# The last norm, the value tiles and the residual of a two-layer graph transformer, emitted as chains of their own

## The chip, the cores and the metric

The kernel runs on one core of a Trainium2 chip. The core has five engines that each work through their own queue in the order in which the program was written: TensorE (PE; weight loads are shown apart as PEld), VectorE (DVE), ScalarE (ACT), GpSimd (POOL) and SyncE (SP), which here only issues DMAs. They wait for each other by semaphores. The metric is the device time of one launch in microseconds; all times below are in microseconds unless they say ns. Samples are processed one after the other on this core; nothing is shared with other cores.

## What is computed

The input has 16 samples of 1024 nodes with 256 features and a 1024 x 1024 adjacency of zeros and ones. Each sample goes through two layers. Cut to what matters:

```python
# layer 0: typed graph attention, 4 heads of 64
h = einsum('bnd,hde->bhne', x, W)
attention = softmax(where(adj == 0, -1e9, leaky_relu(e_src + e_dst)))
dst = einsum('bhij,bhje->bhie', attention, h) + bias
x = layernorm(x + head_norm(relu(dst) + h))
# layer 1: attention with q = k = v, 8 heads of 32, then an MLP
normed = layer_norm(x) * gamma1 + beta1
attn = softmax(where(adj > 0, normed @ normed.T / sqrt(32), -inf))
y = layer_norm(x + attn @ normed) * gamma2 + beta2
x1 = x + attn @ normed
x = layernorm(x1 + gelu(y @ W1 + b1) @ W2 + b2)     # the last norm
```

All of it is in fp32.

## The kernel before

**Two layers side by side.** The kernel is one long straight program that a planner in Python writes out while it runs. Two generators, `layer0` and `layer1`, each emit one sample after the other: layer 0 of sample b+1 is interleaved with layer 1 of sample b. Each `yield` in them says how much work was emitted and what the next piece needs. The main loop picks the stream that comes next: `wanted()` interpolates in `COURSE` (L1095) how far layer 0 should have come for the place that layer 1 has reached, and the loop takes layer 0 while it is behind that target. `WORK0` (L1088) is the sum of work of one sample's layer 0; `SLACK1` and `STAY` (L1093, L1094) say how far the loop may leave the target when the piece at hand would have to wait. A rough clock (`Pace`) estimates when each engine would be free and each tile written; the order is fixed when the program is built.

**A sample's layer 0.** `prepare` projects the nodes in eight blocks of 128. Each is two matmuls acc<-w0e,xT of 128 x 264, which this text calls projection halves; ScalarE then makes a mask out of the adjacency (mask<-ak) and takes four small pieces out of the bank (apart, v, dinv, hb), and VectorE makes z and v. `attention0` (32 steps of two blocks) lets VectorE make weights (p<-cb,dinv,mask) three steps ahead and TensorE multiply them with the values (acc<-v,p, sixteen records per block as an fp32 product is two passes). Its results are read by a chain (`residual0`: a reciprocal, relu, hb), then `after0` normalises.

**A sample's layer 1.** `attention1` has 32 steps. Each makes logits for four heads (ps<-nT, eight records, into the four banks of the pool `ps`), ScalarE takes exponentials out of them (p<-ps, four of 128 x 512), VectorE multiplies by the mask (p<-p,mask, two of 128 x 1024), and three steps later TensorE multiplies by the values v1 (po<-p,v, po<-p,unit, po<-v,p). When the 16 steps of one half of the queries are done, `half_done` starts `finish1` (o<-o,x, statistics, x<-x,o, then ScalarE's o and the transposes to yT). Then `mlp` works in pieces of two blocks: ps<-yT,w_sb, ScalarE's gelu (hid), po<-w_sb,hid; and `last_norm` per block: zz<-po,x on VectorE, after the second block of two the statistics, r on GpSimd (an addition and a power), t on VectorE, zz<-zz,t,r on ScalarE and a store.

**Chains.** Everything that follows a matmul and isn't itself a step is a chain: a generator that stops before each piece that needs something from another engine. `begin` puts it into a list; `advance` runs, between steps, every chain whose needs are met by the rough clock. `complete` runs a chain to its end at once, wherever it stands: its instructions then stand in the queues even if what they read is far from ready.

**What completes a chain early.** A chain is noted as a user of every tile that it takes (`born`) and that it was begun with. When a pool of n buffers hands out a tile for the (n+1)th time, `Ring.tile` (L73) calls `settle` (L450) for the tile whose place it takes, and that completes all chains that use it:

```python
        if len(taken) >= self.bufs:
            self.pace.settle(taken[-self.bufs])
```

So the chain of `last_norm` (L1014) is completed when the pool `po` (two banks) comes back to the bank that its addition read, and the chain of `after0` (L706), which took a bank of `acc` or `ps` for the transposes of normed (its tile is called sq, the transposed one nT), is completed when that bank is taken again. The tail of `after0` behind these transposes makes v1 (a memset and four products, v<-sq,g_r), ratio (two small products) and, 12 us later by the rough clock, the residual x1 (four, x<-sq,ratio,be_r). `half(n)` (L1062) gives `attention1` nT, v1 and x1 of a half of the nodes; if they aren't there it calls `finish_norms` (L1032), which completes all the half's norm chains.

Of the kernel before, what the change touches and what calls it, by code (L numbers as in the profile page):

```python
# [31 lines left out]
F32 = mybir.dt.float32  # L32
# [7 lines left out]
P = 128  # L40
# [150 lines left out]
def fast_path(  # L191
# [24 lines left out]
    nc = Pace(tc.nc)  # L216
    B, N, D = x.shape
    H0, _, HO = w0.shape
# [3 lines left out]
    HD = D // H1  # L222
    NB = N // P
# [4 lines left out]
    BPH = HALF // P  # L228
# [3 lines left out]
    PAIR = 2  # L232
    GB = 2
# [29 lines left out]
    unit = const.tile([P, Q], F32, name="unit")  # L263
# [26 lines left out]
    at = one.tile([P, 3, PAIR, HO, T], F32, name="v0")  # L290
# [38 lines left out]
    def at_time(t):  # L329
        return lambda: t  # L330
# [127 lines left out]
    def begin(chain, engine, *needs):  # L458
        for n in needs:
            if not callable(n):  # L460
                uses(chain, n.tensor.name)
        chains.append([chain, engine, needs])
# [22 lines left out]
    def complete(chain):  # L485

        for item in list(chains):
            if item[0] is chain:
                while item in chains:
                    run(item)  # L490
# [215 lines left out]
    def after0(b, n, hd, o):  # L706


        for first in range(hd + 1):
            complete(residuals[b, n, first])  # L710
        rowwise = [P, BPH, D]
        heads = slice((hd - PAIR + 1) * HO, (hd + 1) * HO)
        oh = o[:, :, heads].rearrange("p g (h e) -> p g h e", e=HO)
        per_head = [P, BPH, PAIR, HO]
        s = small.tile([P, BPH, PAIR], F32, name="s0")
        nc.vector.tensor_reduce(s, oh, axis=mybir.AxisListType.X, op=OP.add)
        nc.vector.scalar_tensor_tensor(
            oh, s[:, :, :, None].to_broadcast(per_head), -1.0 / HO, oh, op0=OP.mult, op1=OP.add
        )
        yield "scalar", o  # L720
        sq = two.tile([P, BPH, PAIR * HO], F32, name="oT1")
        nc.scalar.activation(sq, o[:, :, heads], AF.Square)
        if hd == H0 - 1:
            xl = one.tile(rowwise, F32, name="xl")
            load_x(xl, b, n * BPH, BPH)
        yield "vector", sq
        v = small.tile([P, BPH, PAIR], F32, name="v0s")
        nc.vector.tensor_reduce(
            v, sq.rearrange("p g (h e) -> p g h e", e=HO), axis=mybir.AxisListType.X, op=OP.add
        )  # L730
        r = rstd(v.rearrange("p g e -> p (g e)"), BPH * PAIR, EPS_HEAD * HO, "r0")
        r = r.rearrange("p (g e) -> p g e", e=PAIR)
        pair = o[:, :, heads]
        nc.vector.tensor_mul(pair, pair, lng0_r[:, None, heads].to_broadcast([P, BPH, PAIR * HO]))
        if hd == H0 - 1:
            nc.vector.tensor_add(xl, xl, lnb0_r[:, None, :].to_broadcast(rowwise))
        yield "vector", r
        nc.vector.tensor_mul(oh, oh, r[:, :, :, None].to_broadcast(per_head))
        if hd < H0 - 1:
            return  # L740
        complete(norms[b, n, PAIR - 1])
        nc.vector.tensor_add(o, o, xl)
        yield "vector", o
        mv = small.tile([P, BPH, 2], F32, name="mv0")
        statistics(o, mv, BPH)

        v2 = small.tile([P, 1, BPH], F32, name="v2")
        nc.vector.tensor_scalar(v2[:, 0, :], mv[:, :, 1], 1.0 + EPS, EPS * EPS, op0=OP.mult, op1=OP.add)  # L750
        r2 = power(v2[:, 0, :], BPH, "r2")
        r3 = rstd(mv[:, :, 1], BPH, EPS, "r3")
        yield "vector", r2
        t = minus_mean(mv[:, :, 0], r2, BPH)
        yield "scalar", t
        normed = one.tile(rowwise, F32, name="sq")
        scale_shift(normed, o, t, r2, BPH)
        yield "tensor", normed, side_ready
        nT = two.tile([P, DC, HALF], F32, name="nT")
        for g in range(0, BPH, GB):  # L760
            transpose_rows(nT[:, :, g * P : (g + GB) * P], normed[:, g : g + GB, :], g1_c, be1_c)
            yield "tensor", normed, side_ready
        yield "vector", normed
        v1 = two.tile([P, BPH, H1, HD + 1], F32, name="v1")
        nc.vector.memset(v1[:, :, :, HD], 1.0)
        for g in range(BPH):
            nc.vector.tensor_mul(
                v1[:, g, :, 0:HD],
                normed[:, g, :].rearrange("p (h e) -> p h e", e=HD),
                g1_r.rearrange("p (h e) -> p h e", e=HD),  # L770
            )
        handed[b, n] = [None, v1, nT]
        yield "vector", r3

        ratio = small.tile([P, BPH], F32, name="ratio")
        nc.vector.tensor_mul(ratio, v2[:, 0, :], r2)
        nc.vector.tensor_mul(ratio, ratio, r3)
        yield "vector", ratio, at_time(nc.now() + 12.0)

        x1 = three.tile(rowwise, F32, name="x1")  # L780
        for g in range(BPH):
            nc.vector.scalar_tensor_tensor(
                x1[:, g, :], normed[:, g, :], ratio[:, g : g + 1], be1_r, op0=OP.mult, op1=OP.add
            )
        handed[b, n][0] = x1


    def attention1(half, mask, rinv, half_done, rest):

# [34 lines left out]
                nc.vector.tensor_mul(p, p, mask[n][:, jb, None, :].to_broadcast([P, PAIR, HALF]))  # L826

        def products(quad, jb, ps, moved, held):
            values = half(jb // BPH)[1][:, jb % BPH, :, :]
            for e in range(PAIR):  # L830
                hd = quad * QUAD + e
                for at, v in ((e, values[:, hd, 0:HD]), (PAIR + e, unit)):
                    nc.tensor.matmul(
                        moved[at * Q : (at + 1) * Q, :], v, ps[0][:, e, :], start=jb == 0, stop=jb == NB - 1
                    )
            for e in range(PAIR):
                hd = quad * QUAD + PAIR + e
                for q in range(BPH):
                    for at in range(0, P, Q):
                        nc.tensor.matmul(  # L840
                            held[at : at + Q, q, e, :],
                            ps[1][:, e, q * P + at : q * P + at + Q],
                            values[:, hd, :],
                            start=jb == 0 and e == 0 and q == 0,
                            stop=jb == NB - 1 and e == PAIR - 1 and q == BPH - 1,
                        )
# [167 lines left out]
    def last_norm(b, k, g, po, x1, z, mv, first=None):  # L1014
        if first is not None:
            complete(first)
        nc.vector.tensor_add(z[:, g, :], po, x1)
        if g < GB - 1:
            return
        statistics(z, mv, GB)  # L1020
        r = rstd(mv[:, :, 1], GB, EPS, "r")
        yield "vector", r
        t = minus_mean(mv[:, :, 0], r, GB)
        yield "scalar", t
        scale_shift(z, z, t, r, GB)
        nc.sync.dma_start(out[b, k * P : (k + GB) * P, :].rearrange("(g p) d -> p g d", p=P), z)


    handed = {}
    norms, residuals = {}, {}  # L1030

    def finish_norms(b, n):  # L1032
        for chain in [c for at, c in norms.items() if at[:2] == (b, n)]:
            complete(chain)

    place = [[0, 0.0], [0, 0.0]]

# [18 lines left out]
    def layer1():  # L1056
        rest, ranges = iter(()), None
        for b in range(B):
            place[1][:] = b, 0.0 if b else REST1
            seen, rinv1, mask = handed.pop(b)  # L1060

            def half(n):  # L1062
                if (b, n) not in handed:
                    finish_norms(b, n)
                return handed[b, n]

            yT = [two.tile([P, DC, HALF], F32, name="yT") for _ in range(NH)]
            halves = {}

            def half_done(n, o, heads):  # L1070
                finish_norms(b, n)
                x1 = handed[b, n][0]
                chain = finish1(o, x1, yT[n], heads)
                bias = add_bias2(x1)
                halves[n] = x1, yT[n], chain, bias
                begin(chain, "vector", done(heads), o)
                begin(bias, "vector", at_time(nc.now() + 60.0), x1)

            yield from attention1(half, mask, rinv1, half_done, rest)
            complete(weights_of_later)  # L1080
            rest = yield from mlp(b, halves)
            in_range(seen)
        yield from rest
# [1 line left out]

    WORK0 = NB // GB * 2.25 + 2.0 + NB * H0 * 1.0  # L1088
    REST1 = 3.5 * GB
    ATTN1 = REST1 + 2.0 + 2.5 * (NH * NB * H1 // QUAD)  # L1090
    WORK1 = ATTN1 + NB // GB * (1.75 * FC / 2 + 3.5 * GB) - REST1
    SLACK = 0.083
    SLACK1 = 0.02  # L1093
    STAY = 0.017  # L1094
    COURSE = [(0.0, 1.0), (REST1 + 1.0, 1.0), (ATTN1, 1.31), (WORK1 - 12.0, 2.0), (WORK1, 2.0)]  # L1095

    def wanted():
        b, done = place[1]
# [478 lines left out]
```

## Time and profile before

| what | value |
|---|---|
| median of 3 runs | 3255.43 (3252.06 to 3255.72) |
| device time of the profiled execution | 3255.19 |
| its span from first to last instruction | 3253.4 |
| mean granted TensorE clock | 0.992 |
| mask products p<-p,mask on VectorE | 1024, mean 1220 ns |
| exponentials p<-ps on ScalarE | 2006 and 42 out of other banks, mean 612 ns |
| layer-0 weights p<-cb,dinv,mask on VectorE | 1024, mean 747 ns |
| x<-sq,ratio,be_r (x1) on VectorE | 128, mean 480 ns |
| v<-sq,g_r (v1) on VectorE | 128, mean 412 ns |
| zz<-zz,t,r on ScalarE | 128, mean 601 ns |
| activation table loads | 32, mean 1283 ns |

A row of the profile's groups names the engine, the operation, the tile written and the tiles read, and counts them. In the order of time a line has its start in us from the span's start, its length, and at the end, in brackets, how long the engine sat idle before it and what ended that. A line of several instructions runs from the first one's start to the last one's end. Buffer numbers are left out, so `acc` is either of two banks, `ps` one of four, `po` one of two. Nearly every operation carries the line of one helper (L61), so this text goes by tiles.

### The profile page before, as it was taken

How to read it: one execution, taken by the hardware profiler on the slowest of the kernel's cores; microseconds unless marked ns; L12 is line 12 of the kernel's file. 1: busy time of each engine (PE TensorE's matmuls, PEld its weight loads, DVE VectorE, ACT ScalarE, POOL GpSimd, SP SyncE). 2: the span in 40 equal slices, each digit the busy share in tenths (PEclk: the TensorE clock that was granted, in tenths of full speed). 3: DMA queues.
4: the chain of work that ended last, by engine and by line, in shares of the span. 5: the costliest groups of instructions: out<-in, count | busy, mean ns of one | idle time of the engine just before them, and what ended most of it. 6: DMA issues, size and time to landing. Idle time of an engine off the chain costs nothing.

```text
span 3253.4 us, 147229 instructions
## 1 busy us (share of the span) xinstructions
PE 3168.4 (97%) x67297; PEld 1979.3 (61%) x67297; DVE 2882.5 (89%) x4943; ACT 1961.9 (60%) x4256; POOL 511.3 (16%) x462
## 2 busy tenths in 40 slices
PE   5899999999999999999999999999999999999998
PEld 4557565575756657566575755757566575665745
DVE  5899898998989989898998989989898998989992
ACT  2473846748376583856738466483755838567483
POOL 1202112030110202112030120301102021120300
PEclk9799999999999999999999999999999999999999
DMA  7212202122031221303122031220312213011000
GB/s 169 58 38 59 63 26 67 39 63 52 26 85 21 70 46 32 87 20 73 36 66 56 26 74 33 63 52 25 87 26 68 41 42 80 20 44 21 30 7 16
DMA packets 209447, 163.18 MB, mean 50 GB/s; under 512 B 138480, under 2 KB 189680, under 8 KB 207856
## 3 DMA queue, kind: packets, MB, share of 16 engines
q1 hardware_dynamic: 204640, 119.07, 14.8%
q0 software_dynamic: 2592, 33.56, 5.3%
q8 instruction: 529, 8.67, 1.1%
q10 hardware_dynamic: 1584, 1.05, 0.1%
q14 instruction: 102, 0.84, 0.1%
HBM read 138.68 MB, written 48.50 MB: 58 GB/s over the span
## 4 chain that ended last, share of the span: by engine, by line
PE 75%; DVE 16%; ACT 4%; issue 3%; DMA 1%; POOL 0%; ACTq 0%; SPq 0%; POOLq 0%; DVEq 0%
PE po L61 28%; PE ps L61 28%; PE acc L61 19%; DVE p L61 14%; ACT p L61 2%; ACT o L61 0%; ACT nT L61 0%; DMA cb<-esr 0%; DVE o L61 0%; DVE st L61 0%; ACT zz L61 0%; DVE v L61 0%; DVE hb L61 0%; DVE z L61 0%; DVE relu L61 0%
## 5 line engine op out<-in xcount | busy, mean ns | idle before, releaser
L61 DVE TENSOR_TENSOR p<-p,mask 128x1024 f32<-128x1024 f32 x1024 | 1191.2, 1220 | 6.9 <-ACT p L61 6.9
L61 ACT ACTIVATE p<-ps 128x512 f32<-128x512 f32 x2006 | 1042.4, 612 | 235.9 <-PE ps L61 220.0
L61 DVE SCALAR_TENSOR_TENSOR p<-cb,dinv,mask 128x512 f32<-128x512 f32 x1024 | 709.3, 747 | 8.1 <-DMA cb<-esr 7.8
L61 PE MATMUL ps<-nT 32*128 32x512 f32 x4012 | 647.1, 641 | 2.2 <-ACT p L61 0.4
L61 ACT ACTIVATE hid<-ps,b_sb 128x256 f32<-128x256 f32 x512 | 242.0, 474 | 586.1 <-PE ps L61 586.1
L61 PE MATMUL acc<-v,p 128*64 128x65 f32 x16384 | 563.5, 225 | 31.0 <-DVE p L61 21.9
L61 PEld LDWEIGHTS po<-v,p 128*32 128x32 f32 x32768 | 397.3, 109 | 315.7 <-issue 264.6
L61 PEld LDWEIGHTS acc<-v,p 128*64 128x64 f32 x16384 | 536.7, 140 | 75.1 <-issue 14.4
L61 PE MATMUL po<-p,v 128*32 128x512 f32 x2048 | 543.4, 605 | 1.3 <-DVE p L61 1.3
L61 PE MATMUL po<-p,unit 128*32 128x512 f32 x2048 | 543.5, 605 | 0.0
L61 PE MATMUL po<-w_sb,hid 128*64 128x256 f32 x4096 | 476.2, 380 | 0.0
L61 PE MATMUL ps<-yT,w_sb 128*64 128x256 f32 x4096 | 475.7, 380 | 0.0
L61 POOL TENSOR_SCALAR r<-mv 128x4 f32<-128x4 f32 (+1 forms) x128 | 86.5, 676 | 2057.4 <-DVE mv L61 2019.5
L61 PE MATMUL po<-v,p 128*32 128x33 f32 x32768 | 393.1, 198 | 7.2 <-issue 6.7
L61 PEld LDWEIGHTS po<-w_sb,hid 128*64 128x64 f32 x4096 | 281.3, 137 | 146.3 <-issue 14.5
L61 PEld LDWEIGHTS ps<-yT,w_sb 128*64 128x64 f32 x4096 | 283.6, 137 | 135.4 <-issue 5.2
L61 POOL TENSOR_TENSOR r<-r,mhalf 128x8 f32<-128x8 f32 (+2 forms) x192 | 313.6, 1633 | 16.0
L61 PEld LDWEIGHTS ps<-nT 32*128 32x128 f32 x4012 | 201.9, 183 | 131.7 <-ACT p L61 84.5
L61 PEld LDWEIGHTS po<-p,v 128*32 128x32 f32 x2048 | 77.8, 108 | 321.7 <-issue 143.4
L61 DVE TENSOR_TENSOR z<-hb,bias_r 128x256 f32<-128x256 f32 x128 | 54.2, 423 | 163.8 <-ACT hb L61 163.8
L61 PE MATMUL acc<-w0e,xT 128*128 128x264 f32 x512 | 174.5, 435 | 10.5 <-issue 10.5
L61 ACT ACTIVATE mask<-ak,shift_c 128x1024 uint8<-128x1024 bf16 x120 | 142.1, 1184 | 0.0
(115 smaller groups left out, 2437.7 us busy)
## 6 DMA issues: line engine op xcount, KB each, us to landing
cb<-esr SPq DMA_DIRECT2D x64, 512.0 KB
adjb<-in_adj_dram POOLq DMA_DIRECT2D x30, 1024.0 KB, 11.5
xk<-in_x_dram SPq DMA_DIRECT2D x64, 256.0 KB
xl<-in_x_dram SPq DMA_DIRECT2D x32, 512.0 KB
out_dram<-zz SPq DMA_DIRECT2D x64, 256.0 KB
ak<-adjb SPq DMA_TRANSPOSE x240
ak<-in_adj_dram POOLq DMA_DIRECT2D x8, 256.0 KB, 6.8
w_sb<-in_L_gnn_W_dram SPq DMA_DIRECT2D x2, 1024.0 KB
```

Source lines behind the costliest of these rows:

```text
L61: return method(*args, **kwargs)
```

## The change

The tail of `after0` behind the last transposes of normed becomes two generators of their own, `values1` (v1) and `rows1` (ratio and x1), which `after0` begins when it ends; they took no bank, so no bank that comes back completes them. The hand-over `handed[b, n]` is filled with nT already there, v1 and x1 follow. `attention1` asks for v1 by a function of its own, `values(n)`, when the products need it, and `half(n)` completes only the chain that makes nT. `finish_norms` goes through its list twice, as completing `after0` puts new chains into it. In `last_norm` everything behind the second addition becomes the generator `norm_rows`, begun there with the tile z. The addition of b2 to x1 (`add_bias2`, x<-x,b_r) is due 70 instead of 60 us later by the rough clock, and five constants of the planner change.

```diff
@@ after0 @@
             yield "tensor", normed, side_ready
-        yield "vector", normed
+        handed[b, n] = [None, None, nT]
+        norms[b, n, "values"] = values1(b, n, normed)
+        begin(norms[b, n, "values"], "vector", normed)
+        norms[b, n, "rows"] = rows1(b, n, normed, v2, r2, r3)
+        begin(norms[b, n, "rows"], "vector", normed, r3)
+
+    def values1(b, n, normed):
         v1 = two.tile([P, BPH, H1, HD + 1], F32, name="v1")
...
-        handed[b, n] = [None, v1, nT]
-        yield "vector", r3
-
+        handed[b, n][1] = v1
+        yield from ()
+
+    def rows1(b, n, normed, v2, r2, r3):
         ratio = small.tile([P, BPH], F32, name="ratio")
         nc.vector.tensor_mul(ratio, v2[:, 0, :], r2)
         nc.vector.tensor_mul(ratio, ratio, r3)
         yield "vector", ratio, at_time(nc.now() + 12.0)
...
@@ attention1, products @@
-            values = half(jb // BPH)[1][:, jb % BPH, :, :]
+            v1 = values(jb // BPH)[:, jb % BPH, :, :]
...
@@ last_norm @@
         nc.vector.tensor_add(z[:, g, :], po, x1)
-        if g < GB - 1:
-            return
+        if g == GB - 1:
+            begin(norm_rows(b, k, z, mv), "vector", z)
+        yield from ()
+
+    def norm_rows(b, k, z, mv):
         statistics(z, mv, GB)
         r = rstd(mv[:, :, 1], GB, EPS, "r")
         yield "vector", r
...
@@ finish_norms @@
-        for chain in [c for at, c in norms.items() if at[:2] == (b, n)]:
-            complete(chain)
+        for _ in range(2):
+            for chain in [c for at, c in norms.items() if at[:2] == (b, n)]:
+                complete(chain)
...
@@ layer1 @@
                 if (b, n) not in handed:
-                    finish_norms(b, n)
+                    complete(norms[b, n, H0 - 1])
                 return handed[b, n]
+
+            def values(n):
+                if handed[b, n][1] is None:
+                    complete(norms[b, n, "values"])
+                return handed[b, n][1]
...
-                begin(bias, "vector", at_time(nc.now() + 60.0), x1)
+                begin(bias, "vector", at_time(nc.now() + 70.0), x1)
...
-    WORK0 = NB // GB * 2.25 + 2.0 + NB * H0 * 1.0
+    WORK0 = NB // GB * 2.0 + 2.0 + NB * H0 * 1.0
...
-    SLACK1 = 0.02
-    STAY = 0.017
-    COURSE = [(0.0, 1.0), (REST1 + 1.0, 1.0), (ATTN1, 1.31), (WORK1 - 12.0, 2.0), (WORK1, 2.0)]
+    SLACK1 = 0.01
+    STAY = 0.01
+    COURSE = [(0.0, 1.0), (REST1 + 0.0, 1.0), (ATTN1, 1.32), (WORK1 - 14.0, 2.0), (WORK1, 2.0)]
```

More of the change, by code (lines that the diff above doesn't have):

```diff
@@ L778, in after0 @@
         yield "vector", ratio, at_time(nc.now() + 12.0)
-        x1 = three.tile(rowwise, F32, name="x1")
+        x1 = three.tile([P, BPH, D], F32, name="x1")
         for g in range(BPH):
@@ L785, in after0, with attention1 @@
         handed[b, n][0] = x1
-    def attention1(half, mask, rinv, half_done, rest):
+    def attention1(half, values, mask, rinv, half_done, rest):
         steps = [(n, quad, jb) for n in range(NH) for quad in range(H1 // QUAD) for jb in range(NB)]
@@ L828, in products @@
         def products(quad, jb, ps, moved, held):
-            values = half(jb // BPH)[1][:, jb % BPH, :, :]
+            v1 = values(jb // BPH)[:, jb % BPH, :, :]
             for e in range(PAIR):
                 hd = quad * QUAD + e
-                for at, v in ((e, values[:, hd, 0:HD]), (PAIR + e, unit)):
+                for at, v in ((e, v1[:, hd, 0:HD]), (PAIR + e, unit)):
                     nc.tensor.matmul(
@@ L842, in products @@
                             ps[1][:, e, q * P + at : q * P + at + Q],
-                            values[:, hd, :],
+                            v1[:, hd, :],
                             start=jb == 0 and e == 0 and q == 0,
@@ L1076, in half_done @@
                 begin(chain, "vector", done(heads), o)
-                begin(bias, "vector", at_time(nc.now() + 60.0), x1)
-            yield from attention1(half, mask, rinv1, half_done, rest)
+                begin(bias, "vector", at_time(nc.now() + 70.0), x1)
+            yield from attention1(half, values, mask, rinv1, half_done, rest)
             complete(weights_of_later)
```

## The prediction

> **What bounds the kernel now.** I read the page first (part 1), then the stretches of one sample, then who waits before the tile zz, then the order of time around the places where TensorE is late. The page says
>
> ```profile
> PE 3168.4 (97%) x67297; PEld 1979.3 (61%) x67297; DVE 2882.5 (89%) x4943; ACT 1961.9 (60%) x4256; POOL 511.3 (16%) x462
> ```
>
> TensorE is busy almost always, so only what it waits for, and what its own instructions cost, can move the time. But 97% hides waits: a group of matmuls that is held up half way is still drawn as one long bar. The same chain of starts repeats every 196.8 us (the logits after the MLP start at 321.58 in one sample, and 196.9 later the next one's), fifteen times after the first sample. One such period, cut at its phases:
>
> ```profile
> core 0: us, PE busy (x) PEld busy (x) DVE busy (x) ACT busy (x) POOL busy (x), PEclk, DMA share, GB/s
> 331.50:380.00 48.50, 48.37 (x1108) 24.71 (x1108) 39.02 (x58) 41.44 (x98) 2.57 (x2) 1.00 0.30 63
> 380.00:390.10 10.10, 10.10 (x252) 5.18 (x248) 7.97 (x9) 8.70 (x22) 0.00 (x0) 1.00 0.23 56
> 390.10:440.00 49.90, 48.87 (x1408) 26.44 (x1407) 49.55 (x69) 35.34 (x78) 2.97 (x2) 1.00 0.06 14
> 440.00:518.40 78.40, 78.38 (x1368) 60.93 (x1368) 74.77 (x154) 27.27 (x55) 22.97 (x21) 1.00 0.22 52
> ```
>
> From 331.5 to 390 VectorE has 11.6 us of room and TensorE with ScalarE leads. From 390.1 to 440 VectorE is full (49.55 of 49.90): there it sets the time. In the MLP (440 to 518) TensorE runs without a gap, with VectorE close behind (74.77 of 78.40).
>
> Where TensorE loses time shows in the lengths of the logits group (eight records of ps<-nT). Unhindered it takes 1.14:
>
> ```profile
> 337.71 1.18 PE L61 MATMUL ps<-nT 32*128 32x512 f32 x8
> 340.39 1.16 PE L61 MATMUL acc<-w0e,xT 128*128 128x264 f32 x4
> 341.67 2.58 PE L61 MATMUL ps<-nT 32*128 32x512 f32 x8
> ...
> 362.60 1.77 PE L61 MATMUL ps<-nT 32*128 32x512 f32 x8
> ```
>
> The group at 341.67 is 1.44 too long. All four logits banks must be emptied by ScalarE's exponentials first, and ScalarE did this:
>
> ```profile
> 337.58 1.04 ACT L61 ACTIVATE nT<-acc,be_c,g_c 128x256 f32<-128x256 f32 x2
> 340.04 1.10 ACT L61 ACTIVATE zz<-zz,t,r 128x256 f32<-128x256 f32 x2 [1.41 <-issue]
> 341.04 2.04 ACT L61 ACTIVATE p<-ps 128x512 f32<-128x512 f32 x4
> ```
>
> It sat idle for 1.41 in front of the last norm's zz, with the exponentials of the group of 337.71 behind it. zz waited for VectorE's t, which stood behind v1 and was only done at 339.96:
>
> ```profile
> 338.79 1.09 DVE L61 TENSOR_TENSOR v<-sq,g_r 128x256 f32<-128x256 f32 x3
> 339.80 0.16 DVE L61 SCALAR_TENSOR_TENSOR t<-mv,r 128x2 f32<-128x2 f32 x1
> ```
>
> It is no single case: the list for tile zz, of what its engines sat idle for, has
>
> ```profile
>   issue: 28.0, 15
> ```
>
> that is 1.87 each, once per period. The loss per period, from the lengths of such groups: 0.63 at 321.58 (behind the table load), 1.79 around 341.67 (1.44 and three small ones), 0.63 at 362.60, 1.09 in four groups from 400 to 408, 1.78 at 434 to 440, the last of it behind VectorE's relu:
>
> ```profile
> 440.02 0.69 PE L61 MATMUL acc<-v,p 128*64 128x65 f32 x16 [1.05 <-DVE relu L61]
> ```
>
> Sum 5.9 of 196.8.
>
> **What the Trainium skill says.** "Perfetto Trace Analysis", Per-instruction lifecycle, has ScalarE and VectorE as strict FIFOs; the trace agrees (1.41 idle while four exponentials with full banks stood behind zz). Its section Identifying the Most-Contended Engine calls matmul busy time a poor measure, which the 2.58 group above, counted as busy, bears out. "VectorE: DVE Perf Modes", The perf-mode tier table, gives no faster mode than 1x for an fp32 tensor_tensor; the mask products take 1220 ns for 1024 elements here, so VectorE's 390 to 440 can only be shortened by giving it less to do.
>
> **The change part by part**, per period, against the profiled run (span 3253.4, device time 3255.19; the median of the runs, 3255.43, is the same within 0.01%).
>
> (1) The last norm as a chain from the addition on. Before, taking the next po bank emitted the whole chain, zz and its DMA included, while r was still under way. In the built order of the changed kernel t stands two mask products and one z, v pair after v1, and ScalarE's zz stands one set of exponentials later than before. The 1.41 idle goes. What is late next is ScalarE itself: in an ordinary step (logits to logits 3.29) four exponentials start 1.15 after the group does (354.45 against 353.30), take 1.92 until the next instruction may start (341.04 to 342.95) and so end at about 3.2; 1.37 fits between two sets for nothing. A mask (342.95 to 344.09, 1.14) fits; zz (340.04 to 341.04) with a mask, 2.14, does not, by 0.77. In the changed order zz and a mask do stand together once. So the 1.79 becomes about 0.7: gain 1.1, bounds 0 (the crowd costs as much as the wait did) and 1.79.
>
> (2) v1 and x1 as chains. The same instructions, five and six of 85 to 480 ns; x1 moves from two mask products behind v1 to eight behind it, past 1.9 us (four of 480 ns), into a phase with 11.6 us of room on VectorE. Nothing waits for x1 before the second half of the attention ends. Zero, bounds -0.2 and +0.2. Setting nT in the hand-over earlier lets the first logits of the second half be emitted without v1; they waited for nT only. Zero. The bias addition (1.22) moves within the MLP: zero, as VectorE has 3.6 us there and TensorE no gap; without that cover 1.2.
>
> (3) The new constants. In the changed order every logits group from the second products on has a projection half in front of it, until the projections end; before, two stood in the MLP's tail, and the group at 362.60 had nothing. With nothing in front a step takes 2.63, exponentials end at 3.2, and 0.6 is lost; with 0.64 of projection it isn't. Gain 0.63, bounds 0 and 0.63. A third projection half now lies between 390 and 440, where VectorE sets the time: its instructions there count the same in both orders (26 mask products, 14 weights, one finish, two z, v), so 0.64 less 0.14 for other switches is hidden: gain 0.5, bounds 0 and 0.6.
>
> (4) Finer slices. TensorE's order has 2842 blocks of one kind where it had 2721. A projection half alone takes 0.64 to the next logits, two together 1.09 (389.24 to 390.33), so a split costs 0.20. Sixteen layer-0 products before MLP products take 0.52, ninety-six 2.80 (445.19 to 447.99), 0.466 per sixteen, so a switch costs 0.05. Summing every block of both orders with its unhindered length in this trace gives +8.1 in all (projections +4.3, layer-0 products +5.2, transposes -1.3): a loss of 0.54. Bounds 0.3 and 0.6: inside 390 to 440 some is hidden.
>
> (5) DMAs and queues. The same 64 stores of zz; each follows its zz by about a step on SP's queue, in front of mask transposes whose blocks are three deep. Zero, as no logits wait for a DMA. POOL's r is idle most of the time: zero.
>
> (6) The first sample. Between 119 and 157 us about 14 are lost, with matmuls at half speed after long waits (po<-p,v 1.06 at 133.91 instead of 0.62). The new order has one projection half fewer there. Gain 2, bounds -3 and 6.
>
> Sum: 15 x (1.1 + 0.63 + 0.5 - 0.54) = 25, and 2: 27 us. 3255.2 - 27 gives 3228; I take 3229.
>
> **The rivals.**
> A. The crowd on ScalarE takes the place of the wait: (1) gives nothing. For it: ScalarE is busy 41.44 of 48.50, and zz with a mask goes over by 0.77 at each meeting. Against: the idle time itself is gone. 15 x (0.63 + 0.5 - 0.54) = 9: 3246.
> B. The saved time is handed to VectorE: it is the bound from 390 on, and if its backlog starts earlier but ends when it did, (1) and (3) show only as longer waits at 434 to 440. For it: 49.55 of 49.90. Against: before 390 it has 11.6 us of room and its full stretch begins with hs, which TensorE triggers. Then a gain of 0.5 stands against the 0.54 of (4): 3255, within 0.2%.
> C. Slower: the MLP loses its cover. VectorE makes layer-0 weights only three pairs ahead, and has 3.6 us of room in 78.4. The last norm's statistics and x1's bias now fall among them at other places, and layer-0 products come in twos and threes between MLP pieces. If they wait for weights 2.5 us per period in all, the sum is 15 x (-1.69 + 2.5) = +12: 3267. It decides from 1.7 us per period on. Against: the count of layer-0 products at each point of the MLP is the same at its checkpoints (16 at 7.8 us after the attention, 21 at 13.6, 33 at 27.3 in both orders).
> D. More than forecast: the crowd of (1) fits, and the four groups from 400 to 408 shrink too: 15 x (1.79 + 0.63 + 1.3 - 0.54) = 48: 3207.
> That the change doesn't do what it says is excluded for the order, which shows the later zz and x1.
>
> **How the numbers follow.** Forecast 0.47, A 0.22, B 0.12, C 0.11, D 0.08. A measurement of this kernel tells about 0.2% (6.5 us) from no change. Faster by more: the forecast, D, and A but for 0.03 of it: 0.74. Within: B and that 0.03: 0.15. Slower: C, 0.11. The range runs from half way to D, where (1) reaches its bound, 3212, to B's edge, 3254; the forecast's own is 3215 to 3240.
>
> **What would show it.** Right: zz's idle time "issue" falls from 28.0 to under 5; no logits group of 2.58 in the period, one of about 1.8 instead; none of 1.77 in the middle; 390 to 440 still full on VectorE and just as long; period near 195.1. (3) and (4): the projection half stands before nearly each logits group at 0.64. Wrong: if zz's wait is gone and the period is still over 196.3, A or B holds, told apart by where the waits lie (340 to 350, or 434 to 440); if gaps appear in front of acc<-v,p in the MLP, C.

## The result and the profile after

| | before | after |
|---|---|---|
| median of 5 runs each, taken together | 3255.72 (3252.06 to 3258.22) | 3238.29 (3236.90 to 3238.59) |
| profiled execution, its span | 3255.19, 3253.4 | 3238.05, 3236.2 |
| from the first matmul to the first logits after the first sample | 313.1 | 317.2 |
| mean of the 14 periods after it | 197.19 | 195.82 |
| from the last such logits to the end | 171.2 | 169.3 |

The ratio is 0.9946, 95% interval 0.9932 to 0.9961: faster by 17.4, where 27 was forecast. The profiled executions account for it: 14 x (195.82 - 197.19) = -19.2, the first sample +4.1, the end -1.9, in all -17. Of the 4.1, 3.1 lie ahead of the very first logits (117.3 from the first matmul, 114.2 in before), where TensorE's order is the same in both kernels. In the other runs' profiles the same stretch takes 110.1 to 117.6 (114.1 in e6, whose TensorE order is after's throughout), so these 3.1 are scatter. What may be the change's is in the first sample's own period, 199.89 against 198.95 (200.88 in e6).

A period is again counted from the logits after one MLP to those after the next. In before, ten of the 14 took about 196.9, one 197.3 and three about 198.2; in after all are between 195.58 and 196.15. So a regular period lost 1.05, and 0.3 of the mean is due to the four longer ones.

The page's first part, after:

```profile
PE 3156.3 (98%) x67297; PEld 1970.4 (61%) x67297; DVE 2883.0 (89%) x4943; ACT 1964.6 (61%) x4256; POOL 489.9 (15%) x462
```

VectorE and ScalarE have the same work; TensorE's busy time fell by 12, which is waits that were drawn inside bars. One period of after, cut at its phases:

```profile
core 0: us, PE busy (x) PEld busy (x) DVE busy (x) ACT busy (x) POOL busy (x), PEclk, DMA share, GB/s
327.00:334.00 7.00, 7.00 (x57) 3.87 (x56) 5.43 (x15) 6.99 (x15) 3.15 (x3) 1.00 0.42 145
334.00:392.70 58.70, 58.70 (x1366) 29.38 (x1368) 48.24 (x68) 51.56 (x121) 2.57 (x2) 1.00 0.26 66
392.70:442.90 50.20, 49.23 (x1410) 26.71 (x1406) 49.86 (x69) 34.29 (x74) 2.17 (x2) 1.00 0.08 14
442.90:521.30 78.40, 78.40 (x1374) 60.83 (x1368) 74.47 (x154) 28.42 (x57) 22.59 (x21) 1.00 0.21 53
```

The MLP is as long as it was (78.40). The stretch from the hidden state hs on is still full on VectorE (49.86 of 50.20). The first two rows hold the gain: from the first logits to hs it was 68.56 and is 67.27. ScalarE is full in the first row (6.99 of 7.00), as it was at this place in before (6.99 of 7.00 from 323.2 to 330.2). The list for tile zz, of what its engines sat idle for:

```profile
  PE po L61: 92.3, 52
  DVE t L61: 40.0, 15
  issue: 8.2, 1
```

The one case of "issue" that is left, 8.2, is the last zz of the program, and before has it too. So the 28.0 of before were 8.2 at the end and 14 waits of 1.41, not 15 of 1.87 as the prediction divided them, and the 14 are gone. "DVE t", 2.7 each, lies in the MLP, where ScalarE has room. What took the place of the old wait is seen in TensorE's order of time:

```profile
325.41 1.76 PE L61 MATMUL ps<-nT 32*128 32x512 f32 x8
327.11 1.95 PE L61 MATMUL po<-w_sb,hid 128*64 128x256 f32 x16
328.99 1.57 PE L61 MATMUL ps<-nT 32*128 32x512 f32 x8
...
345.08 1.14 PE L61 MATMUL ps<-nT 32*128 32x512 f32 x8
...
348.35 1.87 PE L61 MATMUL ps<-nT 32*128 32x512 f32 x8
```

and in ScalarE's:

```profile
326.02 1.28 ACT L61 ACT_TABLE_LOAD   x1
327.32 2.07 ACT L61 ACTIVATE p<-ps 128x512 f32<-128x512 f32 x4
329.25 1.10 ACT L61 ACTIVATE zz<-zz,t,r 128x256 f32<-128x256 f32 x2
330.23 2.07 ACT L61 ACTIVATE p<-ps 128x512 f32<-128x512 f32 x4
...
344.86 1.11 ACT L61 ACTIVATE zz<-zz,t,r 128x256 f32<-128x256 f32 x2
345.85 1.16 ACT L61 ACTIVATE mask<-ak,shift_c 128x1024 uint8<-128x1024 bf16 x1
```

The group of 2.58 is gone. At 348.35 stands the meeting of zz and a mask that was forecast: 1.87 instead of 1.14, a loss of 0.73. At 328.99 is a loss that wasn't: 1.57, so 0.43. The first logits need the table load, so their exponentials run until about 329.25, and between the two logits groups TensorE has one MLP piece and no projection half, so it comes back before the banks are empty.

### The profile page after: what moved, and what is told of

It reads as the page before. It is cut to its first block, busy times and chain, and to the rows that moved or that the text cites. A ratio compares the mean times of both kernels' runs of the same rounds, so it can differ in the third digit from the quotient of the medians.

```text
span 3236.2 us, 147123 instructions
## 1 busy us (share of the span) xinstructions
PE 3156.3 (98%) x67297; PEld 1970.4 (61%) x67297; DVE 2883.0 (89%) x4943; ACT 1964.6 (61%) x4256; POOL 489.9 (15%) x462
## 3 DMA queue, kind: packets, MB, share of 16 engines
q10 hardware_dynamic: 1584, 1.05, 0.1%
## 4 chain that ended last, share of the span: by engine, by line
PE 83%; DVE 14%; issue 2%; DMA 1%; ACT 1%; POOL 0%; ACTq 0%; SPq 0%; POOLq 0%; DVEq 0%
PE po L61 32%; PE ps L61 29%; PE acc L61 21%; DVE p L61 11%; DVE o L61 1%; DVE st L61 0%; ACT p L61 0%; DMA cb<-esr 0%; DVE hb L61 0%; DVE x L61 0%; DMA w0e<-in_L_gnn_W_dram 0%; DVE v L61 0%; DVE ranges L61 0%; DVE relu L61 0%; DVE z L61 0%
## 5 line engine op out<-in xcount | busy, mean ns | idle before, releaser
L61 PE MATMUL ps<-nT 32*128 32x512 f32 x4012 | 633.6, 642 | 1.0 <-ACT p L61 1.0
L61 PE MATMUL acc<-v,p 128*64 128x65 f32 x16384 | 575.1, 225 | 27.9 <-DVE p L61 20.1
L61 PEld LDWEIGHTS acc<-v,p 128*64 128x64 f32 x16384 | 550.0, 140 | 82.5 <-issue 15.6
L61 PE MATMUL ps<-yT,w_sb 128*64 128x256 f32 x4096 | 483.5, 380 | 0.0
L61 POOL TENSOR_TENSOR r<-r,mhalf 128x8 f32<-128x8 f32 (+2 forms) x192 | 294.7, 1535 | 16.0
L61 PEld LDWEIGHTS ps<-nT 32*128 32x128 f32 x4012 | 193.4, 183 | 137.3 <-ACT p L61 91.4
L61 POOL TENSOR_SCALAR r<-v0s 128x8 f32<-128x8 f32 x64 | 56.0, 874 | 674.1 <-DVE v0s L61 674.1
```

What stands on the lines that cost most here:

```text
L61: return method(*args, **kwargs)
```

## The experiments

One measure is used throughout: TensorE's stalls per period. Each block of TensorE's instructions of one kind is compared with the unhindered length of such a block (same kind, same size, same kind behind it); what a block takes beyond that, where it is over 0.15, is averaged over some ten periods of the profiled execution. The level depends on which length is taken as unhindered, so only differences between kernels are used. The ratios are to runs of before taken beside each kernel.

| kernel | median | ratio to before, 95% | stalls per period |
|---|---|---|---|
| before, the medians beside the others | 3252.9 to 3255.7 | 1 | 5.99 |
| after | 3238.29 | 0.9946 (0.9932 to 0.9961) | 4.73 |
| e1, last norm alone | 3230.24 | 0.9927 (0.9914 to 0.9941) | 3.96 |
| e2, v1 and x1 alone | 3264.01 | 1.0033 (1.0020 to 1.0045) | 6.60 |
| e3, constants alone | 3314.48 | 1.0177 (1.0160 to 1.0194) | 10.42 |
| e5, norm, v1 and x1 | 3228.89 | 0.9924 (0.9911 to 0.9938) | 4.02 |
| e6, norm and constants | 3238.23 | 0.9954 (0.9940 to 0.9967) | 4.77 |
| e7, norm, course 1.29 | 3274.71 | 1.0067 (1.0053 to 1.0081) | 7.06 |
| e8, norm, course 1.27 | 3240.11 | 0.9961 (0.9947 to 0.9975) | 5.14 |
| e9, after, VectorE later +1.2 | 3254.87 | 1.0006 (0.9997 to 1.0014) | 5.81 |
| e10, after, VectorE earlier +1.2 | 3238.26 | 0.9951 (0.9937 to 0.9965) | 4.76 |
| e11, e5 with a sum on GpSimd | 3257.90 | 1.0010 (1.0001 to 1.0018) | 5.66 |

**e1: the last norm alone**

```diff
-        if g < GB - 1:
-            return
+        if g == GB - 1:
+            begin(norm_rows(b, k, z, mv), "vector", z)
+        yield from ()
+
+    def norm_rows(b, k, z, mv):
```

> Only the last norm is a chain of its own; v1/x1 and the constants are as before. Theory 1 (the wait of ScalarE's zz for t was the cost, and the split takes it away): zz's idle time goes from 28 us to under 5, the logits group of 2.58 us is gone, and the time falls by 8 to 18 us (ratio about 0.996). In the built order the step with the copy hs now also has a projection half in front of it, so its 0.63 us should go too. Theory 2 (the constants carry the gain): within 3 us of before (0.999 to 1.001).

Measured: 3230.24, mean period 195.19. The last norm alone brings more than the whole change. Its TensorE order around the place where after loses 0.43, in the order of time of e1:

```profile
321.56 1.76 PE L61 MATMUL ps<-nT 32*128 32x512 f32 x8
323.26 0.71 PE L61 MATMUL acc<-w0e,xT 128*128 128x264 f32 x2
323.90 1.95 PE L61 MATMUL po<-w_sb,hid 128*64 128x256 f32 x16
325.78 1.14 PE L61 MATMUL ps<-nT 32*128 32x512 f32 x8
```

Here a projection half stands between the first two groups and the second is unhindered. The meeting of zz and a mask costs little too: the two stalls left around it are 0.16 and 0.26 per period. And the 0.63 in the middle of the period, which I had put down to the constants, is gone without them: the planner, whose clock moved with the norm, put a projection half there by itself. The split thus changes the order of TensorE as well, so the 24 that e1 gains are two things: the wait for t, and some 9 (14 x 0.63) from the projection half in the middle. No run has the one without the other.

**e2: v1 and x1 alone**

```diff
-        yield "vector", normed
+        handed[b, n] = [None, None, nT]
+        begin(norms[b, n, "values"], "vector", normed)
+        begin(norms[b, n, "rows"], "vector", normed, r3)
```

> Only v1 and x1 are chains of their own. TensorE's and ScalarE's orders are word for word those of before; only VectorE's differs. Theory 1 (what is moved stands where VectorE has room): within 3 us of before (0.999 to 1.001). Rival (1.9 us of x1 moved off the crowded place shortens the 1.44 us wait there): 5 to 15 us faster (0.9955 to 0.9985).

The orders of TensorE and ScalarE are word for word those of before, and still it is slower by 0.33%. ScalarE's order of time, and then VectorE's:

```profile
1328.48 1.09 ACT L61 ACTIVATE zz<-zz,t,r 128x256 f32<-128x256 f32 x2 [1.75 <-issue]
```

```profile
1327.90 0.16 DVE L61 TENSOR_TENSOR ratio<-v,r 128x4 f32<-128x4 f32 x1
1328.16 0.16 DVE L61 TENSOR_TENSOR ratio<-ratio,r 128x4 f32<-128x4 f32 x1
1328.24 0.15 DVE L61 SCALAR_TENSOR_TENSOR t<-mv,r 128x2 f32<-128x2 f32 x1
```

In before t came right behind v1 and ratio after it (339.87). Now the two ratio products stand in front of t: 0.34 more that zz waits (1.75 against 1.41 at this place), with the exponentials behind it. As TensorE's order is the same, this is the cleanest sign that zz's wait sets the period: the shortest periods are 197.2, and 196.8 in before. Over 14 periods 0.34 makes 4.8 of the 9 lost. Most of the rest stands in five long periods (198.3 to 198.7, the other nine 197.5 in the mean). In these five, and in no other, TensorE's granted clock is 0.50 for 3.4 us just after the late group, here at 0.57 in the mean from 1530 to 1534:

```profile
1527.48 2.58 PE L61 MATMUL ps<-nT 32*128 32x512 f32 x8 [0.46 <-ACT p L61]
...
1530.72 1.06 PE L61 MATMUL po<-p,v 128*32 128x512 f32 x1
```

The matmul of 1.06 takes 0.59 in the next period. So a tiny product costs its time in full when an engine that others wait for has it in its queue, and more where the clock falls after the wait, here in five of 14 periods.

**e3: the constants alone**

```diff
-    WORK0 = NB // GB * 2.25 + 2.0 + NB * H0 * 1.0
+    WORK0 = NB // GB * 2.0 + 2.0 + NB * H0 * 1.0
...
-    SLACK1 = 0.02
-    STAY = 0.017
-    COURSE = [(0.0, 1.0), (REST1 + 1.0, 1.0), (ATTN1, 1.31), (WORK1 - 12.0, 2.0), (WORK1, 2.0)]
+    SLACK1 = 0.01
+    STAY = 0.01
+    COURSE = [(0.0, 1.0), (REST1 + 0.0, 1.0), (ATTN1, 1.32), (WORK1 - 14.0, 2.0), (WORK1, 2.0)]
```

(and 70 for 60 at add_bias2)

> Only the constants (and the 70 us). Theory 1: the wait of zz for t stays (idle about 28 us before zz), the third projection half moves into the stretch in which VectorE sets the time, two steps with nothing in front of the logits remain in the built order at 0.6 us each: between 8 us faster and 4 us slower (0.9975 to 1.001). Theory 2 (the constants carry the gain): 15 to 20 us faster (0.994 to 0.9955).

Neither theory had a loss of 58 (1.77%). ScalarE's zz in e3, TensorE's logits behind it, and the stretch cut into pieces of 4:

```profile
1348.94 1.09 ACT L61 ACTIVATE zz<-zz,t,r 128x256 f32<-128x256 f32 x2 [2.31 <-issue]
```

```profile
1352.15 3.53 PE L61 MATMUL ps<-nT 32*128 32x512 f32 x8 [1.69 <-ACT p L61]
1355.62 1.06 PE L61 MATMUL po<-p,v 128*32 128x512 f32 x1
```

```profile
core 0: us, PE busy (x) PEld busy (x) DVE busy (x) ACT busy (x) POOL busy (x), PEclk, DMA share, GB/s
1346.00:1350.00 4.00, 4.00 (x97) 2.16 (x86) 3.90 (x9) 1.69 (x5) 0.08 (x1) 1.00 0.02 4
1350.00:1354.00 4.00, 2.31 (x8) 1.50 (x9) 3.97 (x7) 4.00 (x12) 0.00 (x0) 0.88 0.37 106
1354.00:1358.00 4.00, 4.00 (x61) 1.18 (x61) 4.00 (x4) 2.64 (x6) 0.00 (x0) 0.50 0.40 91
1358.00:1362.00 4.00, 4.00 (x113) 2.02 (x105) 0.10 (x1) 1.77 (x4) 0.00 (x0) 0.77 0.02 4
```

The wait for zz is still there and longer, a mask follows it directly, and only then come the exponentials whose banks TensorE needs. TensorE waits so long that its granted clock falls to 0.50, and matmuls that take 0.62 elsewhere take 1.06. The three pieces with 0.88, 0.50 and 0.77 miss 3.4 us of full clock, which is 6.8 us at half. The Trainium skill, "TensorE: Matmul & The Clock Gate", What's actually happening, has half rate as the state after an idle window; this trace agrees with the half rate, and doesn't show how long the window is. Twelve of the 14 periods have these 6.8 us, and two have half of it; those two are the shortest (199.98 and 200.17, the median of the others 201.36). If 3.4 us at half clock cost 1.3, the 6.8 cost some 2.6 of the 4.0 by which the mean period is longer than in before: an estimate from two periods. So the constants are harmful with that wait, most of all through the clock; e6 shows that they are harmful without it too.

**e4: the kernel before, once more**

> The kernel before once more, for its trace. In the profile before, 4 of 14 periods were 1.3 us longer than the other ten (198.2 instead of 196.9), which the profile after does not have. If that belongs to the program, the same number of long periods comes again at the same samples; if it is chance of an execution, their number or place differs.

One run, 3257.24, mean period 197.34. Its longest periods (199.77, 197.76, 197.62, 197.51) are, but for one, at other samples than those of the first profile. So they belong to the execution and not to the program. The traces tell in part what makes them. In two of before's three long ones GpSimd's addition r<-mv takes 3.38 instead of 1.11, and VectorE's t waits for r inside the stretch that VectorE fills:

```profile
1974.15 3.38 POOL L61 TENSOR_SCALAR r<-mv 128x4 f32<-128x4 f32 x1 [58.33 <-DVE mv L61]
```

```profile
1978.69 0.17 DVE L61 SCALAR_TENSOR_TENSOR t<-mv,r 128x4 f32<-128x4 f32 x1 [1.25 <-POOL r L61]
```

The addition ends 0.09 after two mask products of VectorE do (1977.44); in a regular period it ends 0.09 after the product x<-x,o. That fits what e11 shows further down, GpSimd and VectorE keeping each other waiting, but no run tried it. In the third long period TensorE sat idle for 1.29 in the middle of a po<-v,p group for nothing that the profile shows, and the 199.77 of e4 has 3.4 us at half clock. Why these fall where they do is open.

**e5 and e6: two parts at a time.** e5 joins the edits of e1 and e2, with the old constants. e6 joins those of e1 and e3.

> The last norm and v1/x1 as chains, old constants. The last norm alone gave 3230.2 us, the whole change 3238.3, v1/x1 alone cost 9 us, with 33.0 instead of 28.0 us of idle time before zz. Theory (v1/x1 cost only because they made zz's wait longer, which is now gone): 3227 to 3234 us, ratio 0.9915 to 0.994. Rival (v1/x1 cost 8 us by themselves, and that is what the whole change gives back): 3236 to 3242 us, ratio 0.9945 to 0.996.

> The last norm as a chain and the new constants, v1/x1 as before. TensorE's order is word for word that of the whole change. Theory (the constants give 8 us back: 0.43 at the second logits and 0.73 where zz meets a mask, per period): 3235 to 3242 us, ratio 0.9945 to 0.996. Rival (v1/x1 give it back): 3227 to 3234 us, ratio 0.9915 to 0.994.

e5, 3228.89, is e1 within their spreads (3227.12 to 3231.91 and 3225.52 to 3231.70): once zz doesn't wait for t where exponentials stand behind it, ratio in front of t costs nothing. e6, 3238.23 (3237.43 to 3239.86), is after. TensorE's order in e5 is that of e1, in e6 that of after. So v1 and x1 are worth nothing, the last norm -24, and the constants give 7 to 9 back (7 by the ratios of e5 and after, 9 by those of e1 and e6). The stalls say it too: 4.77 against 4.02, of which 0.43 is the second logits group. e5 and e1 are the best versions found; e5 is faster than before by 0.76% (0.62 to 0.89) and than after by 7 to 9.

**e7 and e8: another course**, with the last norm's edit and otherwise the old constants.

```diff
-    COURSE = [(0.0, 1.0), (REST1 + 1.0, 1.0), (ATTN1, 1.31), (WORK1 - 12.0, 2.0), (WORK1, 2.0)]
+    COURSE = [(0.0, 1.0), (REST1 + 1.0, 1.0), (ATTN1, 1.29), (WORK1 - 12.0, 2.0), (WORK1, 2.0)]
```

(1.27 in e8)

> The last norm as a chain, old constants, but the course of layer 0 at the end of the attention lowered from 1.31 to 1.29: in the built order one pair of layer-0 weights and products less per period stands before the MLP. Theory (VectorE sets the time of the last 50 us of the attention, and 1.4 us less of its work there shortens the period by up to 1.4): 3205 to 3225 us, ratio 0.985 to 0.991. Rival (the wait is only moved into the MLP, where VectorE has 3.6 us of room): 3227 to 3250 us, ratio 0.9915 to 0.9985.

> The same with 1.27: about two layer-0 pieces less before the MLP. Theory: 3195 to 3220 us, ratio 0.9815 to 0.9895, unless the MLP's room of 3.6 us is used up. Rival: 3230 to 3260 us, ratio 0.9925 to 1.0015, with gaps of TensorE in front of the layer-0 products in the MLP.

1.29 is slower than before (neither the theory nor the rival had that), and 1.27 lies between e1 and before, within its rival's range but without the gaps in the MLP that the rival named. From 1.31 down the time goes up and then down again: it can't be read off the direction of this constant. The profile of e7 has new stalls early in the stretch after hs, in TensorE's order of time and in ScalarE's:

```profile
1390.60 1.77 PE L61 MATMUL ps<-nT 32*128 32x512 f32 x8
...
1397.88 2.44 PE L61 MATMUL ps<-nT 32*128 32x512 f32 x8
```

```profile
1393.68 1.17 ACT L61 ACTIVATE mask<-ak,shift_c 128x1024 uint8<-128x1024 bf16 x1
1394.72 0.22 ACT L61 ACTIVATION_READ_ACCUMULATOR mask<-ak,shift_c 128x1 f32 x1
1395.14 2.08 ACT L61 ACTIVATE o<-o,t,r 128x256 f32<-128x256 f32 x4 [0.20 <-DVE t L61]
1397.12 2.02 ACT L61 ACTIVATE p<-ps 128x512 f32<-128x512 f32 x4
```

A mask and finish1's o, 3.3 together, stand between two sets of exponentials, where the prediction reckoned that 1.37 fits. That this crowd costs the time was read and not tried, and it is not the whole of the loss. At the start of the MLP TensorE also waits for VectorE's relu, for 1.4 to 1.6 in each of the 14 periods:

```profile
1437.39 0.69 PE L61 MATMUL acc<-v,p 128*64 128x65 f32 x16 [1.57 <-DVE relu L61]
```

TensorE's idle time between 105 and 125 us of a period is 2.1 in the mean here and 1.1 in e1, about 1.0 of the 3.0 by which the mean period is longer (198.19 against 195.19). In e8 it is 0.3: less work for VectorE does shorten that wait, as the theory had it, and the time is lost again elsewhere.

**e9 and e10: is the stretch after hs bound by VectorE?** The same idle instruction (x1 against itself by max, so that x1 stays as it is) is put into the kernel after, in the stretch or ahead of it.

```diff
         nc.vector.tensor_add(x1, x1, o)
+        if n == 0:
+            nc.nc.vector.tensor_tensor(x1, x1, x1, op=OP.max)
```

(e9, in finish1; in e10 the same at the end of rows1, with n == 1)

> The kernel after, with one more VectorE instruction for each sample: the normalised rows x1 of the first half against themselves by max (128x1024, in place, the result is what was there; some 1.2 us by its like), issued in finish1 of the first half, which is inside the stretch of about 50 us from the hidden state to the values of head 2 in which VectorE has no gap. Theory (VectorE sets the length of that stretch): each period becomes longer by the instruction's whole duration, 1.1 to 1.3 us, so about +18 over 15 periods, 3250 to 3259, a ratio to before near 1.000. Rival (TensorE sets it, and VectorE is merely full): within 4 of the kernel after, 3234 to 3242.

> The same instruction once for each sample, but issued in rows1 of the second half, in the stretch between the MLP and the hidden state, where VectorE has about 11 us of gaps in each period. Theory (only the later stretch is bound by VectorE): nothing, within 4 of the kernel after, 3234 to 3242. Rival (an instruction of VectorE costs its time wherever it stands, or delays the chain to the hidden state): 10 to 18 more, 3248 to 3257.

e9 has it here, in VectorE's order of time:

```profile
397.32 1.19 DVE L61 TENSOR_TENSOR x<-x,o 128x1024 f32<-128x1024 f32 x1
398.55 1.23 DVE L933 TENSOR_TENSOR x<-x 128x1024 f32<-128x1024 f32 x1
```

+16.6 in e9, or 1.1 for each of 15 periods (the first sample's and the 14), from an instruction of 1.23; its mean period is 197.09 against 195.82, longer by 1.27. In e10 nothing (3238.26, periods 195.80). The stretch from hs to the values of head 2 is bound by VectorE, and the stretch ahead of it is not: shown, at one place in each.

**e11: one instruction less for VectorE there.** On e5, with the planner told as before:

```diff
-        nc.vector.tensor_add(x1, x1, o)
+        if n == 0:
+            nc.enter("vector", "tensor_add", (x1, x1, o), {})
+            nc.nc.gpsimd.tensor_add(x1, x1, o)
+        else:
+            nc.vector.tensor_add(x1, x1, o)
```

> The two split chains of e5 with the old constants, and one instruction of the first half's finish1 (x1 + o, 128x1024, 1.19 us on VectorE, at 398 in the profile of e5) issued on GpSimd instead of VectorE, the order of every other engine as in e5. Theory (VectorE sets the stretch of about 50 us): the stretch becomes shorter by up to 1.2 us, less where TensorE takes over as the bound (it is busy 49.8 of the 50 in it, with some 1.2 us of stalls by the spacing of its groups), so 0.4 to 1.2 for each of 15 periods, 3211 to 3223. Rival (no gain: GpSimd's sum is slow enough to hold up ScalarE's next operation on o, which then waits for it, or the two engines slow each other): 3227 or more.

3257.90, 29 slower than e5, by a mechanism that the rival named only in passing. GpSimd's order of time, then VectorE's:

```profile
393.65 1.85 POOL L61 TENSOR_TENSOR r<-r,mhalf 128x4 f32<-128x4 f32 x1
395.49 2.35 POOL L933 TENSOR_TENSOR x<-x,o 128x1024 f32<-128x1024 f32 x1
```

```profile
393.39 1.22 DVE L61 TENSOR_TENSOR p<-p,mask 128x1024 f32<-128x1024 f32 x1
395.54 2.32 DVE L61 SCALAR_TENSOR_TENSOR t<-mv,r 128x4 f32<-128x4 f32 x1 [0.93 <-POOL r L61]
```

and the same t in e5:

```profile
401.59 0.15 DVE L61 SCALAR_TENSOR_TENSOR t<-mv,r 128x4 f32<-128x4 f32 x1
```

t, of 128 x 4, takes 0.15 in e5 and 2.32 in e11: it ends when GpSimd's sum does. The Trainium skill, "SBUF — State Buffer", Who interferes with whom, has VectorE and GpSimd share a pair of ports by an exclusive lock, and an instruction of VectorE with two inputs in SBUF held up by one of GpSimd that reads there. This trace agrees. VectorE also came to t before r was ready (0.93), since it had one instruction less ahead of it. Together 0.93 + 2.17 - 1.19 = 1.9 more on VectorE, 15 times is 29: what was measured. The stretch took 51.99 against 49.88. So the theory that VectorE sets it holds for a second time, with the other sign than I had wanted.

## Why the forecast held, and where its sum was off

The direction was right, and so was the mechanism of the last norm: zz's wait went and the long logits group with it. 10 of the 27 did not come, and the shares of the parts were wrong. By its terms the last norm was to bring 16 (15 x 1.1) and the constants 9 (15 x (0.63 + 0.5 - 0.54)). Alone the norm brought 24, and the constants took 7 to 9 back. That the total came as near as it did is in part luck.

Two readings were off from the start. zz's 28.0 held 8.2 of the program's end, so the sign "under 5" could not come; what was left is these 8.2. And there are 14 periods between first logits with this wait, not 15, which makes 24 of the 25 in the sum. (Half way from the forecast's 3229 to D is 3218, not 3212.)

**(1), gain 1.1.** For zz it was right to a tenth: 1.79 of stalls became 0.73, the meeting with a mask, forecast at 0.7. But the term left out what the moved zz and the new order would do one step after the table load, 0.43 at 328.99. With it the step gives 0.63. e1, and e6 against it, show that this loss comes from the constants: with the projection half in place the group takes 1.14. Rival A, the crowd on ScalarE, was thus partly true, and at a place that I hadn't named.

**(2), zero.** Right in the change as a whole (e5 against e1), wrong alone (e2, +0.33%). The bound of 0.2 covered five small products of v1 and x1 but not that two of them come in front of an instruction that another engine waits for.

**(3), gain 0.63 and 0.5.** The 0.63 came (the group at 362.38 takes 1.14), but e1 has it without the new constants: the cause was misplaced. The 0.5 did not come: from hs to the values of head 2 it took 49.88 and now 50.21 in the period shown, and 0.1 more in the median of the 14. A stretch that VectorE sets hides a third projection half, as was said, but that buys time only where TensorE would be late elsewhere; and the groups at the start of this stretch lose 1.29 where they lost 1.09.

**(4), loss 0.54.** It was not there. With stalls taken off, TensorE's blocks take as long per period after as before, within 0.1: layer-0 products 31.33 against 31.49, in 28 blocks instead of 24. I had added a switch of 0.05 to the layer-0 products, from a difference between one block of sixteen and ninety-six that already contains its own end. The projections' splits, 0.20 each when read on one pair, cost 0.2 in the sum of a period (9.9 against 9.7), not 0.29.

**(5), zero**: nothing in the runs speaks against it; it wasn't tried alone. **(6), gain 2**: a loss of 4.1 instead, of which 3.1 stands where TensorE's orders are equal, and the first sample's own period, the rest, lost 0.9.

Sum per regular period: -1.06 - 0.63 + 0.43 + 0.2 (groups at the start of the stretch) = -1.06, and -1.05 was measured, where -1.69 was forecast. The projections' 0.2 and the layer-0 products' -0.16 of (4) are left out of it; they nearly cancel. Two wrong terms, the 0.5 that didn't come and the 0.54 that wasn't lost, cancel as well: luck. Over 14 periods the 0.64 that is missing makes 9, the first sample 6 more, and before's long periods, which after hadn't in its profile, give some 5 back: 10, which is the gap.

**The rivals.** B, that VectorE swallows the gain, had the right bound (e9) and the wrong place for it: the full stretch begins with hs, so what is saved ahead of hs moves the whole stretch forward. C, the MLP losing its cover, is out: 78.4 in both. D is out: the crowd did not fit (0.73), and the groups at the start of the full stretch did not shrink.

## What to carry to other kernels

A chain that is completed because its buffer comes back puts its instructions in front of others whose inputs are ready; splitting it where it uses the buffer last takes that wait away. In e1 this edit alone was worth 24, some 9 of it because the planner then laid out TensorE's work better. Constants that steer an order are to be tried again alone after such an edit, since here they lost 58 without it and 7 to 9 with it. Before work is moved off a full engine, look whether that engine is the bound (one idle instruction more, in two places, tells it) and whether the engine that takes the work can run beside it: here GpSimd could not.

## What the runs showed of the hardware that was not expected

- GpSimd's sum of 128 x 1024, 2.35 long, held up a VectorE instruction of 0.15 until its end (e11: t took 2.32 to 2.34; in e5 its longest is 0.165).
- TensorE worked at half clock after some of its waits for the banks of the logits. In e3, where it waited 1.69 and its logits were then held up for 3.53, this happened in all 14 periods, for 6.8 us in twelve of them. In e2, with 0.46 and 2.58, it happened in five of 14, for 3.4 us. In before, whose group of 2.58 has no such idle time in front of it, it happened at this place in none.
- Two executions of one program have periods longer by 1 to 3 us at mostly different samples (before and e4). In two of these periods a GpSimd addition that takes 1.11 elsewhere took 3.38, and in two others the time stands in TensorE (1.29 idle in one, 3.4 us at half clock in the other); no run tells why.
